# The second bias and the mask of a perceptron, moved from VectorE to TensorE and ScalarE in a kernel whose order a planner lays out

## The chip, the cores and the metric

The kernel runs on one core of a Trainium2 chip. The metric is the device time of one execution in microseconds (us). Engines are named as the profile names them: PE is TensorE's matrix products, PEld its weight loads, DVE is VectorE, ACT is ScalarE, POOL is GpSimd, SP is SyncE.

## What is computed

There are 16 graphs of 1024 nodes with 64 features each. Four layers follow each other, and each adds its result to its input and normalises over the features. Layers 0 and 1 multiply features by the adjacency. Layers 2 and 3 take for every node the weighted quantiles of its neighbours' features (they need a sort over the neighbours) and put them through a small perceptron:

```python
def perceptron_layer(x, agg, mask, W1, b1, W2, b2):   # layers 2 and 3
    out = x + agg                                     # agg: weighted quantiles
    h = jax.nn.relu(out @ W1 + b1)                    # 64 -> 128
    y = h @ W2 + b2                                   # 128 -> 64
    return y * mask[..., None]
x = layernorm(x + perceptron_layer(...))
```

The change is in the last two lines of the perceptron: the bias `b2`, the mask, and how the product's blocks leave PSUM.

## The kernel before, in words

A graph's 1024 nodes are 8 tiles of 128. Nodes are sorted by the number of their neighbours, so that each tile's lists have one length. Two graphs make a pair; a round handles one of the two perceptron layers for one pair, so there are 16 rounds. In a round, neighbours' features come by two ways. For the seven lists of moderate length, GpSimd gathers rows from DRAM into a ring of 60 places (`got_s`, `fetch`, L1306). For the longest lists, `fill` (L1036) picks rows on TensorE: a one-hot matrix `hot` of 128x1024, made on VectorE or ScalarE in one of five buffers, is multiplied with the features in three bf16 parts, 24 products into `pgk`, and ScalarE copies every three picked rows to `got`. VectorE sorts the lists by minima and maxima (`exchange`, L1340, tiles `other`, `got_s`, `got`). ScalarE weighs the wanted places and TensorE sums them with products by the identity into PSUM (`weigh`, L1106), from where ScalarE copies them to `agg`.

`finish` (L1162) is the perceptron, called for each of the 16 graphs and both layers, 32 times. Its four steps of two tiles each do: one product of `w1s` with `agg` into `ph`; ReLU on ScalarE with the first bias as its bias, giving `h_t`; two products of `h_t` with `w2s` into `pd`, the same PSUM bank; and on VectorE `y = pd + b2r`, a block of 128x128, with the bias replicated over all rows. After the four steps, VectorE multiplies the whole `y` (128x512) by the mask and adds the layer's input `xc`. `settle` (L510) normalises: sums on VectorE, eight blocks each way on ScalarE. The result of the first perceptron layer is written to a table in DRAM, from which later gathers read; that of the second goes out by eight indirect writes that GpSimd issues. The last two finishes run side by side, one with the PSUM bank `m`, the other (`spare`) with one of two wide banks.

The order of work on VectorE, ScalarE and TensorE is fixed when the program is built[...]. All streams (features, cuts and lists of later graphs, fills, sorts, finishes) are generators that `Weave` (L1217) steps. It keeps a clock for each engine from costs written by hand in `Clocks.cost` (L238): on ScalarE 0.28 us + elements/1200, on VectorE 0.125 us + elements/960 where PSUM is read or two tensors are, an fp32 product 0.05 us + elements x 0.00196. A stream that yields comes back after the planner's time for its last instruction, plus 0.3 us (`SLACK`). So a changed cost or a changed number of yields may move instructions of all other streams.

Of the kernel before, what the change touches and what calls it, by code (L numbers as in the profile page):

```python
# [12 lines left out]
F32 = mybir.dt.float32  # L13
# [5 lines left out]
AF = mybir.ActivationFunctionType  # L19
# [3 lines left out]
P = 128  # L23
# [302 lines left out]
def adj_resnorm_kernel(ctx: ExitStack, tc: tile.TileContext, x, adj_t, nodemask, w01, b01, w02, b02,  # L326
                       w21, b21, w22, b22, w31, b31, w32, b32, out):
    nc = tc.nc
    B, N, C = x.shape
    NT = N // P  # L330
# [9 lines left out]
    dve = Timed(clocks, "DVE", nc.vector)  # L340
    nc = SimpleNamespace(tensor=Timed(clocks, "PE", whole.tensor), scalar=Timed(clocks, "ACT", whole.scalar),
                         gpsimd=Timed(clocks, "POOL", whole.gpsimd), sync=Timed(clocks, "SP", whole.sync),
                         vector=whole.vector, values_load=whole.values_load)

    const = ctx.enter_context(tc.tile_pool(name="const", bufs=1))
# [29 lines left out]
        nc.vector.memset(ends_of[:, i : i + 1], float(value))  # L375
    one_f = const.tile([P, 1], F32, name="one_f")
    nc.vector.memset(one_f, 1.0)
    eps = const.tile([P, 1], F32, name="eps")
    nc.vector.memset(eps, EPS)
    nth = const.tile([P, 1], F32, name="nth")  # L380
# [129 lines left out]
    def settle(dst, y, chain):  # L510

        st = s.work.tile([P, 4, NT], F32, name=f"ln_st_{chain}", bufs=1)
        dve.reduce_sum(st[:, 0], y, axis=AX.X)
        dve.tensor_scalar(st[:, 1], st[:, 0], -1.0 / C, None, op0=ALU.mult)
        yield
        for t in range(NT):
            nc.scalar.activation(y[:, t, :], y[:, t, :], AF.Identity, bias=st[:, 1, t : t + 1])
        nc.scalar.activation(dst, y, AF.Square)
        yield
        dve.reduce_sum(st[:, 2], dst, axis=AX.X)  # L520
        yield
        nc.scalar.activation(st[:, 3], st[:, 2], AF.Sqrt, bias=eps, scale=1.0 / C)
        yield
        dve.reciprocal(st[:, 0], st[:, 3])
        yield
        for t in range(NT):
            nc.scalar.activation(dst[:, t, :], y[:, t, :], AF.Copy, scale=st[:, 0, t : t + 1])
        yield
# [633 lines left out]
    def finish(m, b, e, layer, agg, spare=False):  # L1162

        xc = e.xs[layer]
        w1s, b1c, w2s, b2r = mlps[layer]
        own, wide = ("y_x", "node_in") if spare else ("y_m", "o_t")

        y = s.work.tile([P, NT, C], F32, name="y_m", tag=own, bufs=1)
        own_rows = slice(m * C, (m + 1) * C)
        for g in range(0, NT, 2):  # L1170
            if spare:
                bank = s.psum.tile([P, N], F32, name="m_o", tag="big", bufs=2)
            else:
                bank = s.psum.tile([P, HALF], F32, name="m_o", tag="m", bufs=1)
            ph, pd = bank[:, : 2 * P], bank[:, 2 * P : 3 * P].rearrange("p (g c) -> p g c", c=C)
            nc.tensor.matmul(ph[:H], w1s[own_rows], agg[own_rows, g : g + 2, :], start=True, stop=True)
            yield
            h_t = s.work.tile([H, 2 * P], F32, name="h_t", tag=wide, bufs=1)
            nc.scalar.activation(h_t, ph[:H], AF.Relu, bias=b1c)
            yield  # L1180
            for q in range(2):
                nc.tensor.matmul(pd[:, q, :], h_t[:, q * P : (q + 1) * P], w2s, start=True, stop=True)
            yield
            dve.tensor_add(y[:, g : g + 2], pd, b2r[:, None, :].to_broadcast([P, 2, C]))
        dve.tensor_mul(y, y, e.mask[:, :, None].to_broadcast([P, NT, C]))
        dve.tensor_add(y, y, xc)
        tag, bufs = ("x3s", 4) if layer == 0 else ("x2s", 4) if spare else ("x4s", 1)
        xn = s.feat.tile([P, NT, C], F32, name="xn", tag=tag, bufs=bufs)
        yield from settle(xn, y, "x" if spare else "m")
        yield  # L1190
        if layer == 0:
            nc.sync.dma_start(table[1][b % TABLES][:N, :].rearrange("(t p) c -> p t c", p=P), xn)
            e.xs[1] = xn
            weave.add(parted(b, e, 1))
            return
        for t in range(NT):
            put = nc.gpsimd.indirect_dma_start(
                out=out_rows_of, out_offset=bass.IndirectOffsetOnAxis(ap=e.out_rows[:, t : t + 1], axis=0),
                in_=xn[:, t, :], in_offset=None)
            tc.declare_no_dep(put.ins, group=f"rows{b}", reason="they write different rows")  # L1200
            tc.add_to_no_dep_group(f"rows{b}", put.ins)

    def parted(b, e, layer):

        back = 2 if layer else 3
        while splitting or (b >= back and not entries[b - back].filled[layer]):
            yield
        splitting.add(b)
        parts = s.feat.tile([P, NT, 3, C], BF, name=f"x{layer}p", bufs=back)
        rest = s.feat.tile([P, NT, C], F32, name="rest", bufs=1)  # L1210
        yield from split(e.xs[layer], parts, rest)
        splitting.remove(b)
        e.parts[layer] = parts
# [113 lines left out]
    def finish_round(k, agg, sums):  # L1327
        for gen in sums:
            while weave.runs(gen):
                yield  # L1330
        layer, both = members(k)
        if k < order_of_rounds.index((0, B // 2 - 1)):
            for m, b, e in both:
                yield from finish(m, b, e, layer, agg)
        else:
            ends = [weave.add(finish(m, b, e, layer, agg, m == 1)) for m, b, e in both]
            while any(weave.runs(gen) for gen in ends):
                yield
# [91 lines left out]
    nc = whole  # L1430
# [288 lines left out]
```

## Time and profile before

| | |
|---|---|
| median of three runs | 7080.39 us (7067.44 to 7087.93) |
| time of the profiled execution | 7089.6 us |
| its span, first to last instruction | 7087.9 us |
| granted TensorE clock, mean | 0.721 of full |
| PE busy | 4478.5 us (63%), 51916 products |
| PEld busy | 3422.8 us (48%), 51916 loads |
| DVE busy | 4036.7 us (57%) |
| ACT busy | 3112.9 us (44%) |
| POOL busy | 3090.2 us (44%) |

The profiled execution is 9.2 us (0.13%) above the median and 1.7 us above the slowest of the three runs; another 1.7 us of it lie outside its span. How to read the profile: every recorded instruction is put down to one line, L301, because a helper records them all; so instructions are told apart by their tiles. `y_m` is the perceptron's output block, `m_o` its PSUM bank. An fp32 product appears as two records of PE and two of PEld. "remote" as releaser is an event that the profile puts to no recorded instruction; "issue" is time in which an engine waited for nothing that the profile shows.

### The profile page before, as it was taken

Reading aid. Unit: us, or ns where it says so; the run is one execution under the profiler, and the core shown is the slowest. Engines: PE = TensorE matmul, PEld = TensorE weight load, DVE = VectorE, ACT = ScalarE, POOL = GpSimd, SP = SyncE. Lnnn points to the kernel's source line nnn. Section 1 sums busy time; section 2 is a strip of 40 time slices with the busy share of each in tenths; the row PEclk is TensorE's granted clock in tenths of the full one; section 3 lists DMA queues with packets and bytes.
Section 4 is the critical chain, followed back from the end, with each engine's and each line's share of the span. In section 5 each row is a group of like instructions: output and inputs, shape, how many; then the busy total and the mean of one; then the engine's idle time right before and its main releaser. Section 6 shows DMA issues by size and latency. Waiting matters only on the chain.

```text
span 7087.9 us, 127458 instructions
## 1 busy us (share of the span) xinstructions
PE 4478.5 (63%) x51916; PEld 3422.8 (48%) x51916; DVE 4036.7 (57%) x8753; ACT 3112.9 (44%) x7225; POOL 3090.2 (44%) x3096
## 2 busy tenths in 40 slices
PE   7678676776665767566675656657666566454354
PEld 5446444554544545454544535545555454353344
DVE  2447345574654747556564655638465477375646
ACT  4446444454434445444443444445343444233233
POOL 0432225535254454544455354544445454455540
PEclk8678776776776867777776767768677677666667
DMA  2212212221111211111121211201111010001100
GB/s 79 49 38 60 53 44 49 51 50 20 36 45 24 57 21 46 40 40 41 24 51 29 52 27 30 56 18 39 44 42 32 16 20 16 17 18 21 18 15 5
DMA packets 414449, 253.93 MB, mean 36 GB/s; under 512 B 103434, under 2 KB 365850, under 8 KB 413850
## 3 DMA queue, kind: packets, MB, share of 16 engines
q0 software_dynamic: 96000, 98.50, 7.8%
q1 hardware_dynamic: 317850, 147.19, 7.3%
q8 instruction: 408, 6.68, 0.4%
q14 instruction: 191, 1.56, 0.1%
HBM read 232.88 MB, written 12.59 MB: 35 GB/s over the span
## 4 chain that ended last, share of the span: by engine, by line
PE 41%; issue 21%; DVE 15%; ACT 12%; another core or an unknown queue 9%; POOL 1%; DMA 0%; DVEq 0%; ACTq 0%; POOLq 0%
PE pgk L301 19%; PE pk L301 7%; DVE other L301 6%; DVE got_s L301 4%; PE pa L301 3%; ACT junk L301 2%; ACT hot L301 2%; DVE got L301 2%; PE px L301 2%; PE pr L301 2%; PE m_o L301 2%; ACT got_s L301 2%; PE ordered_x L301 1%; ACT got L301 1%
## 5 line engine op out<-in xcount | busy, mean ns | idle before, releaser
L301 POOL DMA_INDIRECT got_s<-table,idx x2872 | 2948.2, 1027 | 3707.0 <-DVE other L301 1096.4
L301 PEld LDWEIGHTS <-hot 128*128 128x128 bf16 x26304 | 1172.9, 112 | 1686.2 <-issue 1480.2
L301 PE MATMUL pgk<-x1p,hot 128*128 128x64 bf16 x13152 | 709.3, 216 | 692.1 <-issue 499.8
L301 PE MATMUL pgk<-x0p,hot 128*128 128x64 bf16 x13152 | 693.0, 214 | 676.9 <-issue 545.4
L301 DVE TENSOR_SCALAR hot<-place 128x1024 bf16<-128x1024 f16 (+1 forms) x824 | 320.8, 428 | 974.4 <-remote 769.3
L301 PEld LDWEIGHTS <-order 128*128 128x128 bf16 x7008 | 392.1, 105 | 520.0 <-issue 384.9
L301 ACT COPY got<-pgk 64x192 f32<-64x192 f32 (+2 forms) x600 | 182.5, 305 | 994.7 <-PE pgk L301 797.5
L301 ACT COPY agg<-pgk 128x128 f32<-128x128 f32 (+2 forms) x183 | 44.3, 242 | 1164.8 <-PE pgk L301 708.1
L301 PE MATMUL pk<-near,order 128*128 128x512 fp8e4 x1760 | 490.3, 418 | 55.2 <-issue 51.9
L301 DVE TENSOR_TENSOR other<-got_s 128x512 f32<-128x512 f32 (+10 forms) x826 | 491.5, 607 | 13.4 <-DVE hot L301 0.3
L301 PE MATMUL pgk<-ident,got_s 128*64 128x128 f32 x2904 | 425.4, 326 | 89.8 <-ACT got L301 36.2
L301 PEld LDWEIGHTS <-near 128*128 128x128 fp8e4 x4224 | 300.1, 109 | 302.9 <-issue 301.5
L301 PEld LDWEIGHTS pgk<-ident,got_s 128*64 128x64 f32 x2904 | 386.9, 167 | 119.9 <-ACT got L301 41.2
L301 ACT ACTIVATE got_s<-got_s,wts 128x64 f32<-128x64 f32 x1540 | 391.1, 335 | 95.0 <-DVE got_s L301 86.5
L301 DVE TENSOR_TENSOR got_s<-other 128x512 f32<-128x512 f32 (+9 forms) x719 | 391.4, 559 | 8.2
L301 DVE TENSOR_TENSOR got_s<-got_s 128x512 f32<-128x512 f32 (+9 forms) x638 | 373.0, 589 | 20.8 <-ACT got_s L301 5.4
L301 PE MATMUL pa<-x,adj_r 128*128 128x65 f32 x2048 | 331.5, 320 | 78.4 <-issue 70.9
L301 PEld LDWEIGHTS pa<-x,adj_r 128*128 128x128 f32 x2048 | 318.9, 238 | 92.1 <-issue 85.5
L301 ACT ACTIVATE code<-pk,ends_of 128x1024 f16<-128x1024 f32 x220 | 235.4, 1106 | 255.7 <-PE pk L301 113.2
L301 DVE TENSOR_TENSOR other<-other 128x128 f32<-128x128 f32 (+10 forms) x617 | 323.1, 524 | 17.8
L301 ACT ACTIVATE junk<-pr,nb_st 128x1024 fp8e4<-128x1024 f32 x256 | 284.7, 1112 | 72.7 <-remote 34.5
L301 ACT ACTIVATE hot<-hot,one_f 128x1024 bf16<-128x1024 bf16 x272 | 312.3, 1148 | 8.9
(211 smaller groups left out, 7779.9 us busy)
## 6 DMA issues: line engine op xcount, KB each, us to landing
adj_r<-in_adj_dram SPq DMA_DIRECT2D x256, 512.0 KB
got_s<-table,idx POOLq DMA_INDIRECT x2872
x_s<-in_x_dram SPq DMA_DIRECT2D x16, 256.0 KB
table<-x2s SPq DMA_DIRECT2D x16, 256.0 KB
table<-xn SPq DMA_DIRECT2D x16, 256.0 KB
out_dram<-xn,out_rows POOLq DMA_INDIRECT x128
table<-no_row SPq DMA_DIRECT2D x12, 0.2 KB
w21s<-in_L_gnn_W_dram SPq DMA_DIRECT2D x2, 32.0 KB
```

The source lines that it names most:

```text
L301: return call(*args, **kwargs)
```

## The change

A row of ones is kept in SBUF. Ahead of each product of `h_t` with `w2s`, a product of that row (one row by 128 columns, as weights) with the first row of the replicated bias (64 columns) opens the accumulation in the same 64 columns of PSUM, so the bias stands there before the main product is added. ScalarE then copies each tile's 64 columns out, multiplied by that tile's column of the mask. VectorE's four additions and its multiplication by the mask go, and one more yield stands ahead of its addition of the input. The fallback path for graphs with longer lists, which this data doesn't enter, is as before.

```diff
@@ constants
+    ones_row = const.tile([1, P], F32, name="ones_row")
+    nc.vector.memset(ones_row, 1.0)
@@ finish
             for q in range(2):
-                nc.tensor.matmul(pd[:, q, :], h_t[:, q * P : (q + 1) * P], w2s, start=True, stop=True)
-            yield
-            dve.tensor_add(y[:, g : g + 2], pd, b2r[:, None, :].to_broadcast([P, 2, C]))
-        dve.tensor_mul(y, y, e.mask[:, :, None].to_broadcast([P, NT, C]))
+                nc.tensor.matmul(pd[:, q, :], ones_row, b2r[:1], start=True, stop=False)
+                nc.tensor.matmul(pd[:, q, :], h_t[:, q * P : (q + 1) * P], w2s, start=False, stop=True)
+            yield
+            for q in range(2):
+                nc.scalar.activation(y[:, g + q, :], pd[:, q, :], AF.Copy, scale=e.mask[:, g + q : g + q + 1])
+        yield
         dve.tensor_add(y, y, xc)
```

## The prediction, written before the changed kernel was run

> **What bounds the kernel now.** I read the busy times first, then the chain of work that ended last, then the waits of all engines by total, and last the tile `y_m` and the final stage of the timeline. All times are of the profiled execution.
>
> The page, its busy times and the shares of its chain:
>
> ```profile
> PE 4478.5 (63%) x51916; PEld 3422.8 (48%) x51916; DVE 4036.7 (57%) x8753; ACT 3112.9 (44%) x7225; POOL 3090.2 (44%) x3096
> ...
> PE 41%; issue 21%; DVE 15%; ACT 12%; another core or an unknown queue 9%; POOL 1%; DMA 0%; DVEq 0%; ACTq 0%; POOLq 0%
> ```
>
> No engine is full. But TensorE has the most work, and 41% of the chain is its instructions; 21% is "issue", and the list of waits puts nearly all of that to TensorE, between its own instructions. So for some 62% of the span the end follows TensorE.
>
> The waits (engine and tile, releaser, total us, times, longest):
>
> ```profile
> PE pgk L301 <- issue: 1088.6, 1293, 10.1
> ACT got L301 <- PE pgk L301: 887.0, 157, 33.2
> DVE hot L301 <- remote: 769.3, 93, 54.0
> PE pgk L301 <- ACT got L301: 383.2, 140, 29.8
> DVE y_m L301 <- PE m_o L301: 334.9, 66, 25.3
> DVE y_m L301 <- remote: 169.3, 18, 26.3
> PEld L301 <- DVE hot L301: 148.2, 60, 13.5
> ```
>
> VectorE and ScalarE mostly wait for TensorE. The other way round, TensorE waits for ScalarE's copies of picked rows (383.2) more than for VectorE's one-hot matrices (148.2 on its weight loads). The lines on `y_m` are the ones that the change touches: VectorE stands 504 us (334.9 + 169.3) with a bias addition at the head of its queue, because the block isn't there.
>
> The tile `y_m` (min/median/max ns):
>
> ```profile
> L301 DVE TENSOR_TENSOR y_m<-m_o,b22r x64: 271/292/294, 892.7 to 6461.0; 128x128 f32<-128x128 f32 x64
> L301 DVE TENSOR_TENSOR y_m<-m_o,b32r x64: 268/292/294, 1926.5 to 7053.5; 128x128 f32<-128x128 f32 x64
> L301 DVE TENSOR_TENSOR y_m<-y_m,mask_s x32: 691/692/705, 929.5 to 7053.8; 128x512 f32<-128x512 f32 x32
> ```
>
> The final stage's timeline, one step of both last finishes:
>
> ```profile
> 7042.59 0.70 PE L301 MATMUL m_o<-agg,w31s 64*128 64x256 f32 x4
> 7042.69 0.29 DVE L301 TENSOR_TENSOR y_m<-m_o,b32r 128x128 f32<-128x128 f32 x1 [0.15 <-PE m_o L301]
> 7043.38 0.84 ACT L301 ACTIVATE h_t<-m_o,b31c 128x256 f32<-128x256 f32 x2 [1.59 <-PE m_o L301]
> ...
> 7043.91 1.10 PE L301 MATMUL m_o<-w32s,h_t 128*128 128x64 f32 x8 [0.62 <-ACT h_t L301]
> ```
>
> Four products of 64 columns (eight records) take 1.10 us: 0.275 us each.
>
> [...]loads of `none`, 32 rows by 128 columns, take 93 ns, of `hot`, 128 by 128, 112 ns. So a one-row product is not a cheap one. [...]the trace has 335 ns for `got_s<-got_s,wts`, the same form from SBUF, and 2.97 us for twelve in a row, 0.247 each.
>
> **The change part by part.**
>
> *VectorE loses* 128 additions x 0.290 us = 37.1 us and 32 multiplications x 0.693 us = 22.2 us: 59 us. At VectorE's share of the chain (15%), 9 us come off the path.
>
> *TensorE gains* 32 x 8 = 256 one-row products, 512 records of products and 512 of loads: 1% of its instructions. No row of before shows such a product; the nearest is `m_o<-w32s,h_t`, same columns on both sides. From below, 0.275 us (the line above): 70 us. From above, the last such step, at a lower clock, takes 1.97 us for four: 0.49 us, 126 us. All 256 main products have 102.8 us of busy time between them (52.4 + 50.4), 0.40 us each[...]. I take 0.35 us: 90 us. Can it hide? The first of each two stands ahead of a product that waits for the ReLU, but those waits are short (22.7 us in 16 cases), for the planner puts other work there. So I charge the share of the path, 62%: 56 us. Were all of it on the path it would be 90, were it all in waits 0.
>
> *ScalarE gains* 256 copies out of PSUM: 0.247 us from below (in a row), 0.335 from above, 63 to 86 us. They come in twos, (0.335 + 0.247)/2 = 0.29: 74 us. At ScalarE's 12%: 9 us.
>
> *A wait moves.* The 504 us in which VectorE stands before `y_m` go to ScalarE. Behind them on VectorE stood sorts and one-hot matrices; behind them on ScalarE stand copies of picked rows (`got`), which TensorE needs in order to go on. But where VectorE waited it was ahead of TensorE, and next it would meet a one-hot buffer not yet free (769.3 us of such waits already). If nothing comes of it the gain is 0; at VectorE's share of the chain, 15% x 504 = 76 us is the most that I grant. I take 16 us, a fifth, since the steady stages follow TensorE. A loss is not excluded: ScalarE's new wait can lengthen the 383.2 us; I leave 6 us for it in the upper end.
>
> *The tail* is part of these sums, and small. A step there lasts 2.43 us. Three of four bias products lie open (0.8 us) for 4 steps, +3.3 us; VectorE's last multiplication and addition (1 us) go. About +2 us.
>
> *The rest:* one memset of a row at the start, beside loads (under 0.1 us, as the one of `x`); no DMA is added or moved past another queue; gathers and output writes are the same in number, and the output writes go out one behind the other as before.
>
> *The order.* The planner charges 0.30 us for a bias product and 0.33 for a copy, and credits 0.26 and 0.66 for VectorE's. The built order is the same up to the first finish, and shifts from there; the last finish starts after 87,405 of TensorE's instructions, in place of 87,165, just about the added ones, and the end has the same sequence of stages. I see no stage that moves. Such a shift can still cost or save some tens of us: at 9% of the chain, events that the trace doesn't name decide.
>
> *Sum:* 56 + 9 - 9 - 16 = +40 us on a profiled 7089.6, to 7129.6. The median stands 9.2 us lower: 7120 us, 0.56% slower.
>
> **The rivals.**
>
> *VectorE is let go (faster).* The place is the bias addition at the head of VectorE's queue. Where VectorE is held up to 25 us, sorts come late, GpSimd's gathers wait for the ring (`POOL got_s <- DVE other`, 1096.4 us in the trace), and the next sums come late. If most of the 76 us is real, and TensorE's work costs only the low price at the share of its instructions (70 x 0.41 = 29), the sum is 29 + 9 - 9 - 76 = -47: some 7035 to 7045, I say 7040. It decides from the point where the moved wait is worth over 56 us, 11% of its 504. For it: the last fifth of the span, where VectorE is busier than TensorE (889 against 744 us from 5670 on). Against: VectorE's waits for one-hot buffers.
>
> *Hidden work (no change).* TensorE is idle for 37% of the span. If the bias products fall into gaps, PE costs 0 to 15 us, ScalarE's and VectorE's shares cancel, and 7083 results. Against: most idle time is "issue", which comes with its instructions and may grow with them.
>
> *The re-laid order decides*, on either side, by 30 us or more: 7050 or 7130. Nothing in the profile chooses.
>
> **How the numbers follow.** A measurement of this kernel can tell about 0.3%, 21 us. TensorE-bound, 7120: 0.42 (0.38 slower, 0.04 within). VectorE let go, 7040: 0.30 (0.27 faster, 0.03 within). Hidden, 7083: 0.13 (0.09 within, 0.02 each side). Order: 0.15 (0.08 slower, 0.06 faster, 0.01 within). Slower 0.48, within 0.17, faster 0.35. Own range of the forecast: lower 29 + 8 (63 x 12%) - 9 - 16 = +12, 7092; upper, 126 x 0.62 = 78, + 10 (ScalarE, 86 x 12%) + 6 - 9 = +85, 7165. The whole range reaches down past the rival's 7040 by 25 us for the order: 7015 to 7165.
>
> **What would show it.** PE busy up by 70 to 126 us, DVE down by 59, ACT up by 63 to 86; the `y_m <- m_o` wait gone from VectorE and seen on ScalarE; VectorE's waits for `hot` grown by several hundred us. If these last don't grow and POOL's wait for `other` shrinks, the rival was right. A span shorter by over 20 us with PE busy as said makes the prediction wrong: TensorE's share of the chain is then no price for work added to it.

## The result and the profile after

| | before | after |
|---|---|---|
| median | 7084.16 us (4 runs, 7067.44 to 7108.16) | 7211.9 us (4 runs, three of them 7192.41 to 7222.95) |
| profiled execution | 7089.6 us | 7222.95 us |
| its span | 7087.9 us | 7221.1 us |
| granted TensorE clock | 0.721 | 0.715 |

The ratio is 1.0175, interval 1.015 to 1.02: the kernel became slower by some 124 us. One run of after took 10584 us; it is counted in the median and left out of the ratio. The forecast was 7120 us, +40. So the direction was right and the size was not, and the time lies above the range, which ended at 7165.

The busy times of the page of after:

```profile
PE 4677.6 (65%) x52428; PEld 3579.6 (50%) x52428; DVE 3992.8 (55%) x8594; ACT 3167.8 (44%) x7481; POOL 3091.8 (43%) x3096
```

Its waits (engine and tile, releaser, total us, times, longest):

```profile
POOL got_s L301 <- DVE other L301: 1104.7, 73, 77.0
...
DVE hot L301 <- remote: 802.5, 102, 24.8
...
DVE hot L301 <- PE pgk L301: 458.6, 208, 16.6
...
PE pgk L301 <- ACT got L301: 272.6, 117, 29.9
...
ACT y_m L301 <- PE m_o L301: 116.8, 43, 24.8
...
DVE y_m L301 <- ACT y_m L301: 101.5, 15, 30.5
...
PEld m_o L301 <- ACT y_m L301: 89.7, 26, 11.7
...
PE m_o L301 <- ACT y_m L301: 84.1, 26, 11.6
...
ACT y_m L301 <- remote: 72.1, 8, 28.1
```

and two waits of before that the prediction doesn't show:

```profile
DVE hot L301 <- PE pgk L301: 191.7, 108, 20.9
...
PE m_o L301 <- DVE y_m L301: 19.1, 13, 5.6
```

TensorE is busy for 199 us more, where 70 to 126 were forecast. VectorE is busy for 44 us less (forecast 59) and ScalarE for 55 more (63 to 86). The 504 us in which VectorE stood before a bias addition are gone, and ScalarE stands only 189 us (116.8 + 72.1) before its copies. But VectorE's waits before `hot`, the one-hot matrices, grew from 961 us (769.3 + 191.7) to 1261; most of that is put to no recorded instruction ("remote"). GpSimd's wait for VectorE's `other`, whose shrinking would have spoken for the rival, stayed (1096.4 to 1104.7 us). Two waits are new or larger. VectorE waits 101.5 us for ScalarE's last copy before it adds the input. TensorE waits 84.1 us for ScalarE to empty the bank `m_o`, where it waited 19.1 us for VectorE. The chain of waits of this execution breaks off early and can't be used.

The busy time of TensorE on the bank `m_o` alone, in before and then in after (window, its length, PE busy and its records, mean granted clock, DMA share, GB/s; the window reaches past the span, so its clock reads above the span's 0.721 and 0.715):

```profile
0.00:8000.00 8000.00, 213.97 (x768) 0.75 0.14 32
```

```profile
0.00:8000.00 8000.00, 362.85 (x1280) 0.74 0.14 32
```

The 256 added products cost 148.9 us of TensorE, 0.58 us each. The other 50 of the 199 us lie on other tiles, at a mean clock of 0.715 in place of 0.721; no run tells what put them there. The tile `m_o` in after shows their records (min/median/max ns):

```profile
L301 PEld LDWEIGHTS m_o<-b22r,ones_row x256: 181/184/333, 891.3 to 6624.2; 1*128 1x128 f32 x128
L301 PE MATMUL m_o<-b22r,ones_row x256: 257/318/471, 891.3 to 6624.3; 1*128 1x64 f32 x128
L301 PEld LDWEIGHTS m_o<-w22s,h_t x256: 186/189/337, 891.6 to 6624.8; 128*128 128x128 f32 x128
L301 PE MATMUL m_o<-w22s,h_t x256: 262/323/476, 891.6 to 6624.9; 128*128 128x64 f32 x128
```

A product of one row lasts as long as one of 128: 318 against 323 ns a record, its load 184 against 189. These are medians over both clocks, with 128 columns of weights in either.

Why 0.58 and not 0.35? The timeline of the last two finishes in after, TensorE's products alone (start, length, what):

```profile
7165.23 0.43 PE L301 MATMUL m_o<-w32s,h_t 128*128 128x64 f32 x2
7165.60 0.43 PE L301 MATMUL m_o<-b32r,ones_row 1*128 1x64 f32 x2
7165.96 0.43 PE L301 MATMUL m_o<-w32s,h_t 128*128 128x64 f32 x2
7166.32 1.14 PE L301 MATMUL m_o<-agg,w31s 64*128 64x256 f32 x4
7168.02 0.68 PE L301 MATMUL m_o<-b32r,ones_row 1*128 1x64 f32 x2 [0.55 <-ACT h_t L301]
7168.63 0.69 PE L301 MATMUL m_o<-w32s,h_t 128*128 128x64 f32 x2
...
7172.33 0.69 PE L301 MATMUL m_o<-w32s,h_t 128*128 128x64 f32 x2
7172.95 1.23 PE L301 MATMUL m_o<-agg,w31s 64*128 64x256 f32 x4
```

and the granted clock of two stretches of it (the third number from the end):

```profile
7164.87:7166.30 1.43, 1.43 (x9) 1.18 (x8) 0.00 (x0) 0.52 (x2) 0.00 (x0) 1.00 0.00 0
7168.00:7172.90 4.90, 4.88 (x16) 3.99 (x16) 0.00 (x0) 0.85 (x3) 0.00 (x0) 0.50 0.00 0
```

Up to 7166.3 the clock is 1.00, and products follow each other by 0.363 us. From 7168 on it is 0.50, and they follow by 0.617 us. The whole traces of before and after have these two grants and no other. In before, the main products alone took 0.275 us each at clock 1.00 (1.10 us for four); at 0.50 the last step, in before's timeline, took

```profile
7049.68 1.97 PE L301 MATMUL m_o<-w32s,h_t 128*128 128x64 f32 x8 [0.62 <-ACT h_t L301]
```

which is 0.49 each. So I estimate from these steps that an added product costs 2 x 0.363 - 0.275 = 0.45 us at full clock and 2 x 0.617 - 0.49 = 0.74 us at half clock. Of the 1280 records on `m_o` in after's trace, 550 start at clock 0.50 (43%); weighted so, the two prices give 0.57 us, an estimate that meets the 0.58.

Why does each product take longer than the 0.275 us of before? The loads show it; first four products of before, then two of after, all at clock 1.00:

```profile
7043.90 0.97 PEld L301 LDWEIGHTS m_o<-w32s,h_t 128*128 128x128 f32 x8 [1.02 <-ACT h_t L301]
```

```profile
7164.15 0.29 PEld L301 LDWEIGHTS m_o<-b32r,ones_row 1*128 1x128 f32 x2
7164.51 0.30 PEld L301 LDWEIGHTS m_o<-w32s,h_t 128*128 128x128 f32 x2
```

One load lasts 0.18 to 0.19 us. In before eight of them take 0.97 us, so each starts (0.97 - 0.19) / 7 = 0.11 us after the last. In after the two loads of one product are also 0.11 us apart (0.29 - 0.18), but the next product's first load comes 0.36 us after this one's first, 0.25 after its second. So each change between a one-row product and a full one costs 0.14 us more, and an added product brings two changes: 0.28 of its 0.45 us at full clock. At clock 0.50 the medians in the trace are 0.17 us within a product and 0.45 at a change.

Before's own profile had such a change. Its product `none` uses 32 rows and stands among products of `hot` with 128 (loads, at clock 1.00):

```profile
2634.16 0.09 PEld L301 LDWEIGHTS <-none 32*128 32x128 bf16 x1 [0.17 <-issue]
...
2634.29 0.76 PEld L301 LDWEIGHTS <-hot 128*128 128x128 bf16 x24
...
2635.10 0.09 PEld L301 LDWEIGHTS <-none 32*128 32x128 bf16 x1
```

The 24 loads of `hot` start 0.03 us apart, but the first comes 0.13 us after `none`, and the next `none` 0.15 us after the last of them. In before a mere change of tile doesn't do this at clock 1.00: loads of `near` and `takes`, both of 128 rows, follow each other by 0.056 us at the median, as two loads of `near` do. (At 0.50 it is 0.107 against 0.069 us.) That the number of rows is what counts is read from such pairs and not tested: no run changes it alone.

### The profile page after: what moved, and what is told of

Read it like the earlier page. It is cut to its first block, busy times and chain, and to the rows that moved or that the text cites. A ratio compares the mean times of both kernels' runs of the same rounds, so it can differ in the third digit from the quotient of the medians.

```text
span 7221.1 us, 128481 instructions
## 1 busy us (share of the span) xinstructions
PE 4677.6 (65%) x52428; PEld 3579.6 (50%) x52428; DVE 3992.8 (55%) x8594; ACT 3167.8 (44%) x7481; POOL 3091.8 (43%) x3096
## 5 line engine op out<-in xcount | busy, mean ns | idle before, releaser
L301 POOL DMA_INDIRECT got_s<-table,idx x2872 | 2947.9, 1026 | 3710.8 <-DVE other L301 1104.7
L301 PE MATMUL pgk<-x0p,hot 128*128 128x64 bf16 x13152 | 717.4, 216 | 650.8 <-issue 561.5
L301 PE MATMUL pgk<-x1p,hot 128*128 128x64 bf16 x13152 | 679.8, 215 | 536.8 <-issue 387.9
L301 PE MATMUL pa<-x,adj_r 128*128 128x65 f32 x2048 | 358.3, 340 | 61.0 <-issue 57.5
L301 PEld LDWEIGHTS pa<-x,adj_r 128*128 128x128 f32 x2048 | 343.1, 256 | 72.5 <-issue 64.8
L301 DVE MAX8 best<-code 128x8 f16<-128x1024 f16 x234 | 276.3, 1216 | 115.8 <-ACT code L301 109.7
L301 DVE TENSOR_TENSOR other<-other 128x384 f32<-128x384 f32 (+10 forms) x617 | 323.0, 524 | 18.5
L301 PE MATMUL px<-adj_r,x_s 128*64 128x128 f32 x2048 | 303.1, 307 | 30.4 <-issue 26.4
```

What stands on the lines that cost most here:

```text
L301: return call(*args, **kwargs)
```

## The experiments

Two theories were held against each other. *The work*: the added products and copies cost what the trace shows, in whatever order. *The order*: the planner's new laying of all streams costs. A third, *the bank*, is a part of the first: TensorE's next product, the first of the next step, waits until ScalarE has emptied the one bank (84.1 us in the trace of after).

The kernels were measured in groups of up to four, each group on one chip, and the chips differ. On two of them the kernel before took 7209 and 7210 us, near the 7084 of the result; I call these chips A. On the three others it took 4843 to 4846 us, chips B. Each difference below is to the kernel before on the same chip: on chips B between the medians, on chips A, where single runs spread more, from the ratio. Chips A are like the one for which the forecast was made.

How the order was held: the planner is shown the old instruction while another is issued (`clocks.put` shows without issuing; with `clocks.on = False` an instruction is issued unseen). The instruction sequences of TensorE, VectorE and ScalarE were then the same, the exchanged instructions apart. From the third experiment on, the lines that do this are left out of the cuts of code.

**All new work, old order.** As in the changed kernel, but the planner sees the old work:

```diff
             for q in range(2):
+                clocks.on = False
+                nc.tensor.matmul(pd[:, q, :], ones_row, b2r[:1], start=True, stop=False)
+                clocks.on = True
...
+            clocks.put("DVE", "tensor_add", (y[:, g : g + 2], pd, b2r[:, None, :].to_broadcast([P, 2, C])), {})
+            clocks.on = False
+            for q in range(2):
+                nc.scalar.activation(y[:, g + q, :], pd[:, q, :], AF.Copy, scale=e.mask[:, g + q : g + q + 1])
+            clocks.on = True
+        clocks.put("DVE", "tensor_mul", (y, y, e.mask[:, :, None].to_broadcast([P, NT, C])), {})
```

> The changed kernel's instructions, laid out in the order of the kernel before: the planner is shown VectorE's addition and multiplication as before, and the one-row products and ScalarE's copies are put in their places without its knowledge. Theory W (the work itself: 90 us more on TensorE, 74 us on ScalarE, the moved wait) expects what the change gave, a ratio to before of 1.015 to 1.020, some 7190 to 7225 us. Theory O (the re-laid order) expects the prediction's small sum or less, a ratio of 0.998 to 1.006.

> After's instructions in before's order once more, in a call of its own chip. If this is a chip on which before takes 7100 to 7200 us: theory of the work, +90 to +140 us (most of the +125 of the changed kernel); theory of the order, under +60 us. On a chip on which before takes 4843 us: +133 us again.

> After's instructions in before's order. On a chip with before at 7100 to 7200 us: theory of the work, +90 to +140 us; theory of the order, under +60 us. On a chip with before at 4843 us: +131 us, as twice measured.

Measured on chips B: 4976.56 us, ratio 1.0281 (1.0267 to 1.0295), and 4976.51, 1.0275 (1.0258 to 1.0293): +133 and +130 us, more than the 1.015 to 1.020 of the theory of the work. On a chip A: 7349.73, ratio 1.0201 (1.0178 to 1.0224), +145 us (139 between the medians). That is no less than the changed kernel's +124, which was measured on another chip. So on chips A the new work costs that much without any new order; its interval and that of the result (1.015 to 1.02) overlap, so a help or a loss by the new order can't be told there.

**Old work, new order.** The planner is shown the products and copies, and issued are before's instructions.

> The converse: the instructions of the kernel before, in the order that the planner lays out for the changed one. Theory O expects 1.012 to 1.020, some 7170 to 7225 us. Theory W expects no difference from before, 0.997 to 1.003.

> Before's instructions in after's order once more. On a chip with before at 7100 to 7200 us: theory of the order, +80 us or more; theory of the work, -25 to +50 us, as with the three other layings tried there. On a chip with before at 4843 us: +114 us again.

Measured on chips B: 4957.19 us, ratio 1.0237 (1.0223 to 1.0251), and 4949.63, 1.0215 (1.0197 to 1.0234): +114 and +104 us. So on chips B a mere laying anew costs 2%, more than either theory expected. It was not measured on chips A.

**The changed kernel beside them, and the kernel before, on a chip B.**

> The changed kernel itself, beside the kernel before, on the same chip as the runs that are compared with it. If the price of the work (+133 us in the old order) and that of the new order (+114 us with the old work) simply add, it takes about 240 us more than the kernel before. If the two are one loss seen twice (the planner's new order was laid for the new work, and gives back part of what the work costs), it takes 110 to 150 us more. Theory of the bank: its wait of TensorE's second product on ScalarE's taking out is 85 to 130 us, against some 20 before.

> The kernel before, unchanged, for its profile beside the others. On every theory its time is that of the kernel before to within 0.3 per cent; what is wanted is TensorE's wait of m_o on y_m and VectorE's waits, to hold against those of the four kernels that changed one thing.

Measured: 5010.81 us, ratio 1.0345 (1.0331 to 1.0359), +165 us; and 4843.85 us. Neither reading holds: 133 + 114 is 247, and 165 is over the 110 to 150 of the other. There, given the new work, the new order adds some 34 us (5011 against 4977), not 114. TensorE's wait for the bank is 74.7 us, under the 85 to 130 of the theory of the bank.

**Parts of what the planner sees.** The work is before's; the planner is shown the one-row products alone, or ScalarE's copies in place of VectorE's steps, or nothing but one more yield:

```diff
         dve.tensor_mul(y, y, e.mask[:, :, None].to_broadcast([P, NT, C]))
+        yield
         dve.tensor_add(y, y, xc)
```

> The old work, unchanged; the planner is shown the one-row products (which are not issued), so that only the order of the kernel's steps is laid anew. Theory of the tuned order (before's order is one that was found good, and any other laying by the same planner loses about as much as the changed kernel's did): +60 to +150 us. Theory of the wrong price (the changed kernel's order is bad because the planner gives the taking out to ScalarE too late or too early, which this kernel doesn't show it): within 25 us of before.

> The old work, unchanged; the planner is shown ScalarE's taking out in place of VectorE's addition and multiplication, and nothing else of the change. Theory of the tuned order: +60 to +150 us, as with any other laying. Theory of the wrong price (the moved step is what spoils the order): +80 to +130 us here, and little for the other two layings of this call.

> The old work, unchanged; one more place at which the planner may turn to other work (an empty step after the multiplication by the mask), nothing else. Theory of the tuned order: +60 to +150 us. Theory of the wrong price: within 25 us of before, since no instruction and no price is changed.

> The old work with one empty step more for the planner. On a chip with before at 7100 to 7200 us: -23 us again. On a chip with before at 4843 us: if what an order is worth is the same on every chip, -10 to -25 us; if an order is good only for the pace of the engines on one chip, +30 us or more.

Measured on chips A: 7260.29 us, ratio 1.0069 (1.0044 to 1.0094); 7256.92, 1.0062 (1.004 to 1.0085); and the yield 7188.48, 0.9968 (0.9953 to 0.9984). On a chip B the yield took 4861.86, 1.0032 (1.002 to 1.0045). These are +50, +45 and -23 us, and +16 on the chip B. Both theories of the order miss. One that changes no price gains, where a tuned order was to lose 60 us or more; and the two others cost more than the 25 us or less than the 80 that the wrong price allows. (Their intervals, 32 to 68 and 29 to 61 us, just reach the 60 of a tuned order.) The yield gains on one kind of chip and loses on the other, by less than either expectation said. What makes an order good I could not find. The yield alone beats both kernels on chips A, but not on B.

**The bias products alone, old order.** VectorE takes the blocks out; in place of the addition it multiplies by the mask, and later does so once more, so its work is as before and the mask comes in twice. The main product is added to what the bias product left.

```diff
+                nc.tensor.matmul(pd[:, q, :], ones_row, b2r[:1], start=True, stop=False)
-            dve.tensor_add(y[:, g : g + 2], pd, b2r[:, None, :].to_broadcast([P, 2, C]))
+            dve.tensor_mul(y[:, g : g + 2], pd, e.mask[:, g : g + 2, None].to_broadcast([P, 2, C]))
```

Then the same with one product of 128 columns for both tiles:

```diff
+            nc.tensor.matmul(pd, ones_row, b2r[:1, None, :].to_broadcast([1, 2, C]), start=True, stop=False)
```

> Order of before; the one-row products alone are added, and VectorE takes the blocks out as before with a multiplication by the mask in place of the addition of the bias (the mask is multiplied twice). The prediction's term for TensorE is +56 us, a ratio of 1.008; from its bounds 0 to 126 us. Theory W in its strict form, TensorE carrying all of the 125 us, expects 1.015 or more. Theory O expects 1.000 to 1.004, since it holds that the products fall into gaps.

> The bias's product alone, in the old order, as in the run that cost 58 us; but one product of 128 columns for each step in place of two of 64, so 128 one-row products in place of 256. If the cost goes by the number of products (0.23 us each), +29 us, with 20 to 40 us allowed; if it goes by columns, +58 us; if it came from something else that stands in both (VectorE's second multiplication in place of its addition), +58 us too, and then TensorE's busy time would have fallen with nothing gained.

Measured on chips B: 4901.2 us, ratio 1.0119 (1.0104 to 1.0135), +58 us; and 4871.48, 1.0059 (1.0045 to 1.0073), +25 us. TensorE on `m_o` in before on a chip B, then with 256 products, then with 128 wider ones:

```profile
0.00:8000.00 8000.00, 180.25 (x768) 0.91 0.14 32
```

```profile
0.00:8000.00 8000.00, 305.88 (x1280) 0.91 0.13 32
```

```profile
0.00:8000.00 8000.00, 243.08 (x1024) 0.91 0.14 32
```

256 products of 64 columns add 125.6 us, 128 products of 128 columns 62.8: 0.49 us each in both. Half the products, half the time, and 25 of 58 us of loss: the price doesn't go by columns. Whether it goes by products or by changes between one-row and full products stays open, for a step has fewer of both here. An order with both bias products ahead of both main ones would tell; it was not tried. The 0.49 is below the 0.58 of after, where 43% of the records start at clock 0.50: with 256 products on the chip B it is 180 of the 1280 (14%), and the two prices from the trace of after, weighted so, give an estimate of 0.49 us. Of the 125.6 us of TensorE, 58 reach the end, 46%. No expectation met it: the ratio 1.0119 is over the forecast's 1.008 and under the 1.015 of a TensorE that carries the whole loss.

**ScalarE's taking out alone, old order.** ScalarE copies with the mask as scale; VectorE adds the bias to the whole block in place of its multiplication, so the bias isn't masked here. In a second kernel the product writes by turns to two halves of the bank:

```diff
-            dve.tensor_add(y[:, g : g + 2], pd, b2r[:, None, :].to_broadcast([P, 2, C]))
-        dve.tensor_mul(y, y, e.mask[:, :, None].to_broadcast([P, NT, C]))
+            for q in range(2):
+                nc.scalar.activation(y[:, g + q, :], pd[:, q, :], AF.Copy, scale=e.mask[:, g + q : g + q + 1])
+        dve.tensor_add(y, y, b2r[:, None, :].to_broadcast([P, NT, C]))
```

```diff
-            else:
+            elif not g:
                 bank = s.psum.tile([P, HALF], F32, name="m_o", tag="m", bufs=1)
+            at = 2 * P + (0 if spare else g // 2 % 2 * P)
-            ph, pd = bank[:, : 2 * P], bank[:, 2 * P : 3 * P].rearrange("p (g c) -> p g c", c=C)
+            ph, pd = bank[:, : 2 * P], bank[:, at : at + P].rearrange("p (g c) -> p g c", c=C)
```

> Order of before; ScalarE takes the blocks out with the mask as scale, VectorE adds the bias to the whole block in place of the multiplication by the mask, so it loses only the 128 additions out of PSUM, and the bias isn't masked. No one-row products. The prediction has +9 us for ScalarE, -6 for VectorE, -16 for the moved wait: 0.998 (0.990 to 1.004). The rival of a VectorE that is let go expects 0.988 to 0.993. If ScalarE's copies of picked rows suffer behind the moved wait, 1.004 or more.

> ScalarE takes out and VectorE adds the bias to the whole block, in the old order, as in the run that cost 67 us; but the second product writes by turns to two halves of the bank, so that the next one need not wait until ScalarE has taken the last one out. Theory of the bank (TensorE waits for ScalarE's queue): most of the 67 us goes, so +25 us or less beside the kernel before, and TensorE's wait of m_o on y_m falls from 122 us to under 30 us. Theory of ScalarE's time (its own 74 us, and VectorE's wait for its last copy, are what costs): the 67 us stays within 15 us, whatever the wait of TensorE does.

> ScalarE takes out and VectorE adds the bias to the whole block, old order. On a chip with before at 7100 to 7200 us: theory of the bank (TensorE's wait for ScalarE costs), clearly more than the +42 us of ScalarE's masking in SBUF, so +65 us or more; theory of ScalarE's time, within 15 us of those +42. On a chip with before at 4843 us: +67 us again.

Measured on chips B: 4910.29 us, ratio 1.0145 (1.0129 to 1.016), +67 us, and again 4912.08, 1.0135 (1.011 to 1.0161); with two halves 4919.62, 1.0149 (1.0134 to 1.0165), +74 us. The waits on `m_o` and `y_m` of before on a chip B, of the first kernel, and of the one with two halves:

```profile
DVE y_m L301 <- PE m_o L301: 125.8, 47, 23.1
...
PE m_o L301 <- DVE y_m L301: 42.5, 24, 6.6
```

```profile
DVE y_m L301 <- ACT y_m L301: 154.3, 27, 18.0
...
PE m_o L301 <- ACT y_m L301: 122.4, 52, 8.3
```

```profile
DVE y_m L301 <- ACT y_m L301: 159.7, 27, 19.6
...
PE m_o L301 <- ACT y_m L301: 122.5, 51, 8.4
```

The forecast's terms for this part were +9, -6 and -16 us, a ratio of 0.998; VectorE let go was to give 0.988 to 0.993. Both fail: VectorE was let go, and the kernel lost 67 us. It did not come by a longer wait of TensorE for `got`, which the forecast feared (334.5 us in before on a chip B, 287.2 here).

TensorE's wait for the bank trebles (42.5 to 122.4 us), and the two halves leave it as it is (122.5): in this program the wait holds for the bank (or for the tile that fills it) and not for the addresses in it. What the chip does without such a wait no run here shows. So this edit did not take away what it was to take away, and says nothing on what the wait costs. A second bank was not tried.

The products (+58) and the taking out (+67) add up to 125 us, all the new work to 130 and 133. So on chips B the loss in the old order is these two parts, about half each.

**ScalarE masks in SBUF, old order.** VectorE takes out and adds as before; only the mask goes to ScalarE:

```diff
-        dve.tensor_mul(y, y, e.mask[:, :, None].to_broadcast([P, NT, C]))
+            for q in range(2):
+                nc.scalar.activation(y[:, g + q, :], y[:, g + q, :], AF.Copy, scale=e.mask[:, g + q : g + q + 1])
```

> The old order; VectorE takes the products out of PSUM and adds the bias as before, and ScalarE multiplies by the mask afterwards, in SBUF, in 256 instructions in place of VectorE's 32. So ScalarE has the same 256 instructions more as in the run that cost 67 us, and VectorE waits for the last of them, but TensorE's next product waits for VectorE and not for ScalarE. Theory of the bank: TensorE's wait of m_o on y_m is 40 to 60 us as before, and the time +25 us or less. Theory of ScalarE's time and of VectorE's wait for it: +50 us or more.

> ScalarE masks in SBUF, VectorE takes out, old order. On a chip with before at 4843 us: theory of the bank, +25 us or less, with TensorE's wait of m_o on y_m near the 42 to 48 us of before; theory of ScalarE's time and VectorE's wait for it, +50 us or more. On a chip with before at 7100 to 7200 us: +42 us again.

Measured on chips A: 7255.59 us, ratio 1.0058 (1.0041 to 1.0075), and 7243.58, 1.0061 (1.0038 to 1.0084): +42 and +44 us (47 and 33 between the medians). TensorE's wait for the bank is 25 and 26 us, with 19 in the profile of before. So 256 more instructions on ScalarE cost even where TensorE doesn't wait for them, more than the 25 us of the theory of the bank. The 50 us of its rival are not excluded (the intervals reach 54 and 61 us). ScalarE also stands in this kernel before VectorE's addition (111.5 and 129.3 us), while in the changed one it stands before TensorE's products.

This kernel and all the new work ran on one chip A, in one order; they differ by 106 us between the medians. The waits of the first, then of the second:

```profile
DVE hot L301 <- remote: 729.1, 95, 55.0
...
DVE y_m L301 <- PE m_o L301: 364.4, 68, 26.9
...
DVE y_m L301 <- remote: 260.6, 22, 22.3
...
DVE hot L301 <- PE pgk L301: 139.5, 97, 11.4
...
DVE y_m L301 <- ACT y_m L301: 88.6, 28, 17.0
...
PE m_o L301 <- DVE y_m L301: 26.3, 14, 6.8
```

```profile
DVE hot L301 <- remote: 923.5, 113, 55.1
...
DVE hot L301 <- PE pgk L301: 329.2, 158, 24.0
...
DVE y_m L301 <- ACT y_m L301: 282.9, 28, 30.4
...
PE m_o L301 <- ACT y_m L301: 82.3, 33, 13.4
```

and their shares of the chain that ended last:

```profile
PE 41%; issue 24%; DVE 16%; ACT 11%; another core or an unknown queue 7%; POOL 0%; DMA 0%; DVEq 0%; ACTq 0%; POOLq 0%; SPq 0%
```

```profile
PE 44%; issue 21%; ACT 12%; DVE 12%; another core or an unknown queue 10%; DMA 0%; POOL 0%; DVEq 0%; SPq 0%; ACTq 0%; POOLq 0%
```

VectorE is let go before `y_m`: 431 us less (713.6 to 282.9). But it stands 384 us longer before `hot` (868.6 to 1252.7). TensorE's instructions on the chain grow, and VectorE's share shrinks from 16 to 12%. So most of the freed wait came back as another. The two kernels also differ by the one-row products, which can delay VectorE's next wait; on chips A no run parts the two.

## Why the forecast was right in direction and wrong in size

*What bounds the kernel* fits what was seen, but is not shown alone: all the new work, which takes 59 us off VectorE, lengthened the kernel on chips A by 145 us, and no run there adds work to TensorE only.

*Two steps failed*, TensorE's price and what the taking out by ScalarE does.

*TensorE's price* is the sentence "I take 0.35 us: 90 us", with 0.49 us as its upper end. The term measured 148.9 us in the changed kernel and 142.5 in the new work in the old order (359.0 against 216.5 with the mask in SBUF). Both ends had been read from main products that follow each other. At full clock the load of a one-row product next to full ones starts 0.14 us later, and so does that of the full one behind it; and 43% of the records start at half the clock, where by my estimate an added product costs 0.74 us. With the share of the path left as it was, 62%, the right size gives 92 us in place of 56. The sum is then +76 us, 7156, still inside the forecast's range and some 50 us short of the result. What part of the products reached the end on chips A was measured only together with the taking out of PSUM: some 100 us (106 by the medians, 1.40% by the ratios). On chips B the products alone cost 58 us, close to the forecast's 56; that is luck, for their price was too low and the share of 62% too high (46% there).

*The taking out by ScalarE* was the larger miss where it was measured alone. The forecast has for the whole of it +9 for ScalarE, -9 for VectorE and -16 for the moved wait, a gain of 16 us. On chips B, where VectorE keeps an addition, the gain was to be 13 us and the loss was 67. On chips A the nearest run, with the mask alone on ScalarE, lost 42 to 44 us, although VectorE lost 22 us of work. ScalarE's duration was right: the forecast took 0.29 us, between the 0.247 and 0.335 of before's trace, and copies took 308 ns at the median from PSUM (after) and 335 from SBUF (the mask in SBUF). So the average share of 12% was no price for it. What makes it dear is in part argued: VectorE stands 101.5 us in after (282.9 in the old order) for the last copy, and TensorE 84.1 us (82.3) for the bank.

*The moved wait*, granted 16 us of gain and at most 76, gave none that can be seen: much of what left `y_m` came back before `hot`, the wait that the forecast had named as the evidence against. The rival "VectorE is let go" fell with it, and so did "hidden work". (That rival's sum of -47 gives 7033 us, not the 7040 that is said.) The upper end left 6 us for a longer wait of ScalarE's users; it named TensorE's wait for `got`, which in fact fell (383.2 to 272.6). It did not name that TensorE, with its next product right behind, waits for ScalarE to empty the bank (19.1 to 84.1 us). How much of the loss that wait is stays open.

*VectorE's* -9 us for 59 us of work can't be seen alone; its busy time fell by 44 us.

*The tail* was put at +2 us. From the first product of the last two finishes to the last instruction of their `xn` it took 23.5 us before (7040.2 to 7063.7) and 34.8 after (7162.2 to 7197.0): +11. The clock falls to 0.50 at 7046.8 in before, 6.6 us after that first product, and at 7166.4 in after, 4.2 us after it; in before the rest of the third step and the last come behind that, in after the last three of the four steps, each with four products more.

*The order*: no stage moved, as forecast, and the layings of the old work that were tried on chips A moved the time by -23 to +50 us, about the size that its rival gave. For the changed kernel itself it can't be told from nothing there. On chips B it adds some 34 us.

What remains open: how the 100 us between the two kernels of one chip A divide into products, taking out and waits for the bank; what the taking out costs by itself on chips A; why an order that costs 114 us with the old work adds 34 with the new.

## What to carry to other kernels

A bias product of one row is a whole product (318 against 323 ns a record), and here, between full products, it came dearer than that: by my estimate 0.45 us at full clock, where a main product had taken 0.275. Look in the trace for what a change of rows does to the next load (here it started 0.14 us later), and price the product at the granted clock at which it will run (here 0.74 us at 0.50, an estimate). A busy time times a share of the chain is no price for work whose end other engines wait for. When an engine's wait is moved away, look first at the next wait of the same engine; if that one follows the bounding engine, little may come of it. When another engine takes a block out of PSUM, ask what stands in that engine's queue ahead of it and whether the next product writes to the same bank (here TensorE's wait for `m_o` grew from 19.1 to 84.1 us).

## What the runs showed of the hardware

The chips differ far more than the change. The kernel before, unchanged, took 4843.85 us on a chip B and 7089.6 in the profiled execution on the chip of the result. VectorE's busy time is the same (4024.0 and 4036.7 us), TensorE's 3801.2 and 4478.5. The mean granted clock is 0.851 on the chip B and 0.721 on the other. What differs most is the time in which TensorE's loads wait for nothing that the profile shows; first the chip of the result, then the chip B:

```profile
PEld L301 <- issue: 2421.7, 3077, 15.9
```

```profile
PEld L301 <- issue: 524.3, 1103, 8.0
```

On that chip B VectorE is busy for 83% of the span and TensorE for 79%, so what bounds the kernel need not be the same there. No run here tells why the chips differ.
